# A list scheduler that gives TensorE the units whose inputs have been ready for a while

## The chip, the core and the metric

One Trainium2 chip (trn2), one of its cores, everything in float32. The metric is the device time of one execution in microseconds (us), as the median of several runs. PE is TensorE's matmul side, PEld its weight loads, DVE is VectorE, ACT is ScalarE, POOL is GpSimd, SP is SyncE, which here only issues DMAs.

## What is computed

The input x has 4 x 1024 tokens of 256 channels. It is normalized, and two branches are added to it:

```python
xn = layernorm(x)                                   # (4, 1024, 256), no scale or shift
# branch 1: linear attention with 16 heads of 16, chunks of 128 tokens, and 4 fixed memories
q, k, v = (split(xn @ w.T) for w in (w_q, w_k, w_v)); sq, sk = elu(q) + 1, elu(k) + 1
local  = causal chunked attention: ((sq sk^T * mask) v + sq S) / clip(its row sums), S += sk^T v
coarse = (sq @ sum(memories)) / clip(sq @ sum(norms))
fine   = sum over m of softmax_m(mean over tokens of sq @ norm_m) * (sq @ memory_m) / clip(sq @ norm_m)
p      = sigmoid(w2 @ relu(w1 @ coarse + b1) + b2)  # one number for each token
attn   = (gate * (p * fine + (1 - p) * coarse) + (1 - gate) * local) @ w_o.T
# branch 2: mixture of 8 experts of width 176, the two best of each token, and a shared MLP of width 352
scores = softmax(xn @ gate_weight.T); w = the two largest, divided by their sum
y      = sum over the two of w * (silu(xn @ wg_e.T) * (xn @ wu_e.T)) @ wd_e.T + shared MLP(xn)
out = x + attn + y
```

## The kernel before

**Stages.** The 4096 tokens are 8 blocks of 512 and 32 tiles of 128. First all blocks are normalized, transposed and turned into values and router logits (lines 328 to 416, up to about 54 us). Then the router picks two experts for each token and sorts the token-expert pairs by expert into 71 slot tiles of 128 (`route`, `sort`, lines 419 to 569). The sorted list is inverted with one-hot matmuls: 22 batches, each `invert` (DVE, L581 and L585), `hold` (ACT, L598) and `hold_weights` (POOL, L608), then `add_slots` (PE, tile `found`, L617). The buffers of a batch come from rings of three, so batch k waits for the `add_slots` of batch k-3. After the last batch `inverted` (DVE, L627 to L633) writes the tables `islot` and `wslot`.

**A round of attention,** for token tile n: `scores` (PE, L746, into the tile `quad`), `mask` (4 times DVE, L753), `memory` (PE, L889, into `quad` again), `weigh` (DVE, L899 to L904) and `fine` (2 times DVE, L923), `gate_coarse` (POOL, tile `cg`, L916), `sum_fine` (POOL: three additions, tiles `fm` and `diff`, L936 to L940), `local` (PE, tile `pn`, L772), `local_copy` (ACT, tile `nT`, L784), `back` (PE, tile `pb`, L793 and L799), `weigh_local` (DVE, tile `loc`, L813 to L817), `base` (POOL, `loc`, L827), `update` (PE, L860), `state` (DVE, L872), `add_state` (POOL, L880); then the gate: `turned` (PE, tile `pt2`, L950), `gate_hidden` (PE, tile `ph`, L976), `gate_sum` (DVE, L985 and L987), `gate_out` (ACT, L993 to L996), `blend` (POOL, tile `o`, L1002), and `output` (PE, tile `po`, L1071 and L1075). Beside the rounds run the projections (L649) and the shared MLP (`pg` L1010, `psu` L1030). Once for each of the 4 sequences `batch_weights` makes the softmax over the memories: 4 small matmuls (L695), then a dozen short DVE and ACT operations (L700 to L719); `weigh` reads its result `w5`.

**The expert part,** for slot tile j: `fetch_rows` (POOL, an indirect DMA that gathers 128 rows, tile `xg`, three buffers, L1133), `fetch_weights` (SP, three DMAs, three buffers), `expert_turn` (PE, tile `pte`, L1166), `turn_copy` (ACT, L1173), `expert_hidden` (PE, tile `phe`, L1183), `expert_tanh` (ACT, L1195), `expert_silu` (DVE, L1200 to L1205), `expert_out` (PE, tile `pye`, L1215), `expert_y` (ACT, L1224), `put` (POOL, an indirect DMA that adds 128 rows to `sums` in HBM, L1229).

**The end.** When the last `put` has landed, `residual` and `experts_part` load `sums` (SP). For tiles 0 to 23 `total` (POOL, L1113, 12 of two tiles each) adds them to what `output` left, and `store_two` (SP) stores; for tiles 24 to 31 `output` runs at the very end, with `output_sum` (DVE, L1083) and `store_one` (a DMA that ACT issues, L1117).

**What sets the order.** PE's main work, some 686 units, is first written as a list (`order`): the rounds, with projections, shared MLP and experts mixed in by weight. A unit's place in it is its due time. `plan` (L1357 to L1584) then runs a list scheduler at build time: every function has an engine and an estimated duration (`cost`), a lag until others see its result (`lag`, `landing`), the units that it must wait for (`needs`), and the PSUM banks (a ring of 4) and `wide` tiles (a ring of 3) that it takes. At each step it looks at the first unit of each function, finds for each engine the one with the smallest rank, and calls the one that begins first. The order of those calls is the order of the instructions on every engine, since each engine works its queue in order. A PE unit may not run more than 12 us ahead of the list (`window`). The estimates act on the order alone. The chip keeps its own time, and a unit that is called too early holds up all that is behind it on its engine.

The heart of it before:

```python
ready = max((done[w] for w in waits if w is not None), default=0.0)
begin = max(ready, free[engine])
rank = (begin, due if engine == "PE" else ready)
```

Of the kernel before, what the change touches and what calls it, by code (L numbers as in the profile page):

```python
# [15 lines left out]
NT = 4  # L16
# [6 lines left out]
def linear_attention_moe_kernel(  # L23
# [53 lines left out]
    BPB = S // TB  # L77
# [118 lines left out]
    for e in range(E):  # L196
# [5 lines left out]
        base=0, pattern=[[1, P]], channel_multiplier=-1,  # L202
# [5 lines left out]
        base=0, pattern=[[1, P]], channel_multiplier=-1,  # L208
# [5 lines left out]
        base=0, pattern=[[-HD, HC]], channel_multiplier=1,  # L214
# [3 lines left out]
        base=HD - 1, pattern=[[HD, HC]], channel_multiplier=-1,  # L218
# [14 lines left out]
    spare = count[:, P + 2 * NTT : P + 2 * NTT + 1]  # L233
# [1123 lines left out]
    def plan(order):  # L1357
# [12 lines left out]
            scores: ("PE", 1.10), memory: ("PE", 0.85), local: ("PE", 1.05), back: ("PE", 0.92),  # L1370
            update: ("PE", 0.48), turned: ("PE", 0.45), keys_back: ("PE", 0.45),
            output: ("PE", 2.17), gate_hidden: ("PE", 0.47), project: ("PE", 1.73),
            shared_gate: ("PE", 1.73), shared_up: ("PE", 1.73), batch_weights: ("PE", 3.50),
            expert_turn: ("PE", 0.24), expert_hidden: ("PE", 1.36), expert_out: ("PE", 0.95),
            odd_keys: ("ACT", 0.52), turned_copy: ("ACT", 0.57), keys_copy: ("ACT", 0.62),
            output_copy: ("ACT", 0.40), local_copy: ("ACT", 0.60), gate_out: ("ACT", 0.90),
# [3 lines left out]
            gate_sum: ("DVE", 0.50), blend: ("POOL", 0.78), weigh_local: ("DVE", 1.08),  # L1380
            state: ("DVE", 0.43), projected: ("DVE", 0.74), shared_silu: ("DVE", 0.66),
            shared_hidden: ("DVE", 0.66), expert_silu: ("DVE", 1.00), mean_queries: ("DVE", 1.30),
            gate_coarse: ("POOL", 0.78), sum_fine: ("POOL", 2.80), base: ("POOL", 0.78),
            add_state: ("POOL", 0.80), put: ("POOL", 1.62), fetch_rows: ("POOL", 1.02),
            fetch_weights: ("SP", 0.3), invert: ("DVE", 1.15), hold: ("ACT", 1.00),
            hold_weights: ("POOL", 0.72), add_slots: ("PE", 0.75), inverted: ("DVE", 0.65),
# [11 lines left out]
        def needs(f, n, *more):  # L1398
# [8 lines left out]
                scores: lambda: qs + ks + [(odd_keys, n), (fine, n - 1, NC - 1)],  # L1407
                mask: lambda: [(scores, n), (local, n - 1)],
                memory: lambda: [(mask, n, g) for g in range(NG)],
                weigh: lambda: [(memory, n), (turned, n - 2), (gate_coarse, n - 1)],  # L1410
                gate_coarse: lambda: [(weigh, n), (base, n - 1), (sum_fine, n - 1)],
                fine: lambda: [(weigh, n), (sum_fine, n - 1)],
                sum_fine: lambda: [(fine, n, NC - 1), (gate_coarse, n), (gate_out, n - 2)],
# [66 lines left out]
        rings = {"bank": [None] * 4, "wide": [None] * 3}  # L1480
# [10 lines left out]
        def taken(f, key):  # L1491

            if f is add_slots:
                return ("bank", (inverted, 0)) if key[1] == 0 else None
            if f not in gives_back or f is update and (state, *key[1:]) not in known:
                return None
            ring, last = gives_back[f]
            if f is output and key[1] >= held_from:
                last = output_sum
            return ring, (last, *key[1:])  # L1500

        def longest_free(ring):

            slots = [(-1.0 if u is None else called[u], k)
                     for k, u in enumerate(rings[ring]) if u is None or u in called]
            return min(slots)[1] if slots else None

        queues, due, place, ended = {}, 0.0, 0.0, False
# [29 lines left out]
        known = {op[0] for queue in queues.values() for op in queue}  # L1538
        queues = {f: queue[::-1] for f, queue in queues.items()}
        free = dict.fromkeys(lag, 0.0)  # L1540
        done, called = {}, {}
        window = 12.0
        while any(queues.values()):
            limit = window + min(
                (q[-1][3] for f, q in queues.items() if q and cost[f][0] == "PE"), default=0.0
            )
            best = {}
            for f, queue in queues.items():
                if not queue:
                    continue  # L1550
                key, args, due, place = queue[-1]
                engine = cost[f][0]
                if engine == "PE" and place > limit:
                    continue
                waits = [key for key in needs(*key) if key in known]
                takes = taken(f, key)
                if takes:
                    slot = longest_free(takes[0])
                    if slot is None:
                        continue  # L1560
                    waits += [rings[takes[0]][slot]]
                if any(w is not None and w not in done for w in waits):
                    continue
                ready = max((done[w] for w in waits if w is not None), default=0.0)
                begin = max(ready, free[engine])
                rank = (begin, due if engine == "PE" else ready)
                if engine not in best or rank < best[engine][0]:
                    best[engine] = rank, f
            assert best
            rank, f = min(best.values(), key=lambda b: b[0][0])  # L1570
            begin = rank[0]
            key, args, *_ = queues[f].pop()
            engine, took = cost[f]
            takes = taken(f, key)
            if takes:
                rings[takes[0]][longest_free(takes[0])] = takes[1]
            called[key] = len(called)
            if f is update and (state, *key[1:]) not in known:
                took = 0.0
                done[add_state, *key[1:]] = begin  # L1580
                called[add_state, *key[1:]] = len(called)
            free[engine] = begin + took
            done[key] = begin + took + landing.get(f, lag[engine])
            f(*args)  # L1584


# [98 lines left out]
    for n in range(held_from, NTT):  # L1685
        order += [(1280, output, n, True), (10, store_one, n)]
    planned.append(True)
    plan(order)


# [54 lines left out]
```

## Time and profile before

| | us |
|---|---|
| median of 3 runs (654.38 to 657.39) | 654.52 |
| the profiled execution | 651.07 |
| its span, first to last instruction | 649.4 |
| PE busy | 627.6 (97%) |
| PE weight loads busy | 487.9 (75%) |
| DVE busy | 429.5 (66%) |
| POOL busy | 408.6 (63%) |
| ACT busy | 278.5 (43%) |
| longest groups: L1183 `phe` matmuls / L1215 `pye` / L1071 `po` | 108.0 / 77.9 / 47.0 |
| POOL: scatter L1229 / gather L1133 / first addition of `sum_fine` L936 | 112.6 / 71.4 / 48.2 |

A row of the timeline gives start, duration, engine, line, operation, what is written from what, shapes and a count of merged instructions, and in brackets the idle time before it and what ended it. A float32 matmul stands as two instructions. Ends of matmuls are modelled, so PE shows as busy also where it runs slowly; the distance from the start of one unit to the start of the next is the better measure of what a unit costs.

### The profile page before, as it was taken

The numbers are of one execution on the slowest core, as the hardware profiler recorded it, in microseconds if no ns is written. First come the engines' busy times: TensorE is split into PE (matmuls) and PEld (weight loads), VectorE is DVE, ScalarE is ACT, GpSimd is POOL, SyncE is SP. The second block draws the span as 40 slices with busy tenths as digits, with TensorE's granted clock in tenths as the row PEclk, the third lists the DMA queues.
The fourth block names the chain that finished last, engine by engine and source line by source line (L and its number), as shares of the span: only waits on it lengthen the run. The fifth ranks groups of instructions, "written<-read, shape, count | busy, mean of one in ns | idle before, by whom it ended". The sixth has DMA issues, their size and how long they took to land.

```text
span 649.4 us, 15187 instructions
## 1 busy us (share of the span) xinstructions
PE 627.6 (97%) x5510; PEld 487.9 (75%) x5510; DVE 429.5 (66%) x1205; ACT 278.5 (43%) x676; POOL 408.6 (63%) x456
## 2 busy tenths in 40 slices
PE   4999999989999999999999999999999999999996
PEld 3884467778888877777786777788888886778775
DVE  6837999966665566566656765666655656667751
ACT  3765455444444454334533444333445434344320
POOL 5310055677777876565665665677777498586876
PEclk9999999999999999999999999999999999999999
DMA  9779000156566753443443444346666675564278
GB/s 301 242 238 248 0 1 2 50 168 166 133 152 144 164 129 87 106 107 77 109 118 78 106 107 98 89 106 138 154 151 160 149 161 127 147 164 99 26 225 301
DMA packets 94379, 86.51 MB, mean 133 GB/s; under 512 B 12033, under 2 KB 91905, under 8 KB 94177
## 3 DMA queue, kind: packets, MB, share of 16 engines
q1 hardware_dynamic: 78976, 65.34, 34.5%
q0 software_dynamic: 13632, 18.62, 16.6%
q10 hardware_dynamic: 1696, 1.58, 0.7%
q8 instruction: 44, 0.72, 0.5%
q14 instruction: 31, 0.25, 0.1%
HBM read 67.56 MB, written 23.59 MB: 140 GB/s over the span
## 4 chain that ended last, share of the span: by engine, by line
PE 89%; DVE 6%; ACT 1%; DMA 1%; issue 1%; POOL 0%; DVEq 0%
PE phe L1183 14%; PE pye L1215 11%; PE po L1071 6%; PE psu L1030 6%; PE pg L1010 5%; PE quad L746 5%; PE pn L772 5%; PE pv L407 5%; PE po L1075 4%; PE quad L889 4%; PE pq L649 3%; PE pk L649 3%; PE pte L1166 3%; PE pb L793 2%; PE pb L799 2%; PE found L617 2%
## 5 line engine op out<-in xcount | busy, mean ns | idle before, releaser
L1229 POOL DMA_INDIRECT sums<-y,islot x71 | 112.6, 1585 | 56.5 <-ACT y L1224 16.1
L1183 PEld LDWEIGHTS phe<-turned,wgu 128*128 128x128 f32 (+1 forms) x852 | 102.2, 187 | 14.9 <-issue 12.9
L1183 PE MATMUL phe<-turned,wgu 128*128 128x128 f32 (+1 forms) x852 | 108.0, 276 | 0.0
L1133 POOL DMA_INDIRECT xg<-xns,islot x71 | 71.4, 1006 | 58.0 <-PE pte L1166 43.9
L753 DVE TENSOR_TENSOR sT<-quad,causal 128x512 f32<-128x512 f32 x128 | 79.4, 682 | 21.9 <-PE quad L746 9.5
L1215 PE MATMUL pye<-wdn,hidden 112*128 112x256 f32 (+1 forms) x284 | 77.9, 396 | 0.5
L1200 DVE SCALAR_TENSOR_TENSOR the<-the,phe 128x256 f32<-128x256 f32 x71 | 29.5, 415 | 43.3 <-ACT the L1195 30.0
L1215 PEld LDWEIGHTS pye<-wdn,hidden 112*128 112x128 f32 (+1 forms) x284 | 48.8, 190 | 11.4 <-issue 3.2
L936 POOL TENSOR_TENSOR fm<-fm 128x512 f32<-128x512 f32 x32 | 48.2, 1506 | 4.2 <-DVE fm L923 4.2
L1224 ACT ACTIVATE y<-pye,wslot 128x256 f32<-128x256 f32 x71 | 33.4, 471 | 38.9 <-PE pye L1215 36.2
L1195 ACT ACTIVATE the<-phe 128x256 f32<-128x256 f32 x71 | 27.1, 382 | 51.6 <-PE phe L1183 45.8
L608 POOL TENSOR_TENSOR held<-ones,two 128x213 f32<-128x213 f32 (+1 forms) x22 | 16.3, 748 | 49.5 <-DVE ones L581 49.5
L1071 PE MATMUL po<-wd,h 128*128 128x256 f32 (+1 forms) x192 | 47.0, 380 | 0.0
L1010 PE MATMUL pg<-xnT,wg 128*128 128x512 f32 (+1 forms) x96 | 45.7, 598 | 0.5 <-DVE th L1040 0.5
L1030 PE MATMUL psu<-xnT,wu 128*128 128x512 f32 (+1 forms) x96 | 45.9, 600 | 0.0
L923 DVE TENSOR_TENSOR fm<-quad,rw 128x512 f32<-128x512 f32 x64 | 41.0, 682 | 0.2
L1071 PEld LDWEIGHTS po<-wd,h 128*128 128x128 f32 (+1 forms) x192 | 35.5, 190 | 6.1 <-issue 1.6
L916 POOL TENSOR_TENSOR cg<-coarse,gates 128x256 f32<-128x256 f32 x32 | 30.9, 964 | 13.9 <-DVE coarse L904 11.6
L1173 ACT COPY turned<-pte 128x256 f32<-128x256 f32 x71 | 26.5, 373 | 27.6 <-PE pte L1166 25.6
L1002 POOL TENSOR_TENSOR o<-o,loc 128x256 f32<-128x256 f32 x32 | 29.7, 929 | 7.8 <-ACT o L996 5.8
L772 PE MATMUL pn<-sT,va 128*32 128x128 f32 x1024 | 34.6, 276 | 0.0
L827 POOL TENSOR_TENSOR loc<-loc,cg 128x256 f32<-128x256 f32 x32 | 26.5, 827 | 12.7 <-DVE loc L817 12.0
(200 smaller groups left out, 1329.8 us busy)
## 6 DMA issues: line engine op xcount, KB each, us to landing
wdn<-in_w_down_dram SPq DMA_DIRECT2D x71, 224.0 KB
wgu<-in_w_gate_dram SPq DMA_DIRECT2D x71, 176.0 KB
wgu<-ups SPq DMA_DIRECT2D x71, 176.0 KB
xns<-x SPq DMA_DIRECT2D x8, 512.0 KB
sums<-in_x_dram SPq DMA_DIRECT2D x8, 512.0 KB
x<-in_x_dram SPq DMA_DIRECT2D x7, 512.0 KB
part<-sums SPq DMA_DIRECT2D x12, 256.0 KB
out_dram<-acc SPq DMA_DIRECT2D x12, 256.0 KB
```

Source lines behind the costliest of these rows:

```text
L649: nc.tensor.matmul(pq, w[:, k, c * P : (c + 1) * P], xnT[:, k, :], start=(k == 0), stop=(k == NC - 1),)
L753: nc.vector.tensor_mul(sT, quad[:, g, :].rearrange("p (c t) -> p c t", t=P), causal[:, None, :].to_broadcast([P, NC * 2, P]),)
L772: nc.tensor.matmul(pn[CW * r : CW * (r + 1), q, :], wide[:, i, first : first + CW], st["sT", h // 2][:, c * 2 + h % 2, :], start=True, sto ...
L923: nc.vector.tensor_mul(fm[:, c].rearrange("p g m (r k) -> p g (m r) k", k=HD), quad[:, :, c * KM + KX + KN : (c + 1) * KM].rearrange("p g ...
L936: nc.gpsimd.tensor_add(fm[:, :, 0:2, :], fm[:, :, 0:2, :], fm[:, :, 2:4, :])
L1010: nc.tensor.matmul(pg[:n, :], wg[:, k, f * P : f * P + n], xnT[:, k, :], start=(k == 0), stop=(k == NC - 1),)
L1030: nc.tensor.matmul(pu[:n, :], wu[:, k, f * P : f * P + n], xnT[:, k, :], start=(k == 0), stop=(k == NC - 1),)
L1071: nc.tensor.matmul(po[:, :H], st["h", blk, f][:k, tok], wd[:k, f, :], start=(f == 0), stop=False)
L1133: nc.gpsimd.indirect_dma_start(out=xg, out_offset=None, in_=xns, in_offset=bass.IndirectOffsetOnAxis(ap=islot[:, j : j + 1], axis=0),)
L1183: nc.tensor.matmul(ph[: cols.stop - cols.start, s, :], wgu[:, k].rearrange("p g f -> p (g f)")[:, cols], xgT[:, k, :], start=(k == 0), sto ...
L1215: nc.tensor.matmul(py[:, :H], hT[:n, f, :], wdn[:n, f, :], start=(f == 0), stop=(f == 1))
L1229: nc.gpsimd.indirect_dma_start(out=sums, out_offset=bass.IndirectOffsetOnAxis(ap=islot[:, j : j + 1], axis=0), in_=st.pop(("y", j)), in_of ...
```

## The change

Three things are changed, all in `plan`, so no instruction is added or removed; only their order on the engines moves.

1. Estimates: `batch_weights` counts 0.95 us of PE in place of 3.50, and DVE is held for its result plus 2.2 us, at which time it is done; `weigh` now waits for it. `sum_fine` counts 3.20 us of POOL in place of 2.80.
2. The rank of a PE unit: its begin is taken as no earlier than the time at which its inputs have been ready for a while. "A while" depends on the engine that made the input (`spare`: ACT 0.4, DVE 0.6, POOL 1.5, SP 1.0 us). Among units with the same begin the earlier due one wins, as before.
3. Once a unit is chosen, its begin is worked out anew from its inputs and the ring slot, without the margin.

```diff
-            shared_gate: ("PE", 1.73), shared_up: ("PE", 1.73), batch_weights: ("PE", 3.50),
+            shared_gate: ("PE", 1.73), shared_up: ("PE", 1.73), batch_weights: ("PE", 0.95),
...
-            gate_coarse: ("POOL", 0.78), sum_fine: ("POOL", 2.80), base: ("POOL", 0.78),
+            gate_coarse: ("POOL", 0.78), sum_fine: ("POOL", 3.20), base: ("POOL", 0.78),
...
-                weigh: lambda: [(memory, n), (turned, n - 2), (gate_coarse, n - 1)],
+                weigh: lambda: [
+                    (memory, n), (batch_weights, n // (BPB * NT)), (turned, n - 2), (gate_coarse, n - 1)
+                ],
...
-        done, called = {}, {}
+        done, called, by = {}, {}, {}
+
+        spare = {"PE": 0.0, "ACT": 0.4, "DVE": 0.6, "POOL": 1.5, "SP": 1.0}
...
                 begin = max(ready, free[engine])
-                rank = (begin, due if engine == "PE" else ready)
+                rank = (begin, ready)
+                if engine == "PE":
+                    safe = max((done[w] + by.get(w, 0.0) for w in waits if w), default=0.0)
+                    rank = (max(begin, safe), due)
...
             rank, f = min(best.values(), key=lambda b: b[0][0])
-            begin = rank[0]
...
+            waits = [w for w in needs(*key) if w in known]
             if takes:
-                rings[takes[0]][longest_free(takes[0])] = takes[1]
+                slot = longest_free(takes[0])
+                waits += [rings[takes[0]][slot]]
+                rings[takes[0]][slot] = takes[1]
+            begin = max([free[engine]] + [done[w] for w in waits if w])
...
             done[key] = begin + took + landing.get(f, lag[engine])
+            by[key] = spare[engine]
+            if f is batch_weights:
+                free["DVE"] = max(free["DVE"], done[key]) + 2.2
+                done[key] = free["DVE"]
             f(*args)
```

## The prediction

> **What bounds the kernel now.** I read the busy times first, then PE's own waits, then the timeline where waits lie, and last the end of the run.
>
> ```profile
> PE 627.6 (97%) x5510; PEld 487.9 (75%) x5510; DVE 429.5 (66%) x1205; ACT 278.5 (43%) x676; POOL 408.6 (63%) x456
> ```
>
> PE works 97% of the span, so the sum of its work (the same after the change) sets the time, and an order of units can win only what PE waits. The waits of PE, by the engine that ended them (total, times, longest, in us):
>
> ```profile
> PE pt L385 <- ACT x L367: 8.7, 2, 7.6
> PE pb L793 <- ACT nT L784: 2.4, 2, 1.2
> PE pte L1166 <- DMA xg<-xns,islot: 2.2, 2, 1.4
> PE pte L1166 <- issue: 1.1, 1, 1.1
> ```
>
> The first line is the start, before the planner's part. The rest, with four waits of 0.5 or less, is 7.0 us (2.4 + 2.2 + 1.1 + 1.2): all that this change could take away. The stages, with PE's busy time as the second number:
>
> ```profile
> 80.00:130.00 50.00, 49.37 (x411) 35.32 (x410) 47.41 (x103) 26.03 (x82) 27.05 (x34) 1.00 0.06 17
> 130.00:200.00 70.00, 67.72 (x694) 57.50 (x693) 45.52 (x126) 29.18 (x71) 53.97 (x55) 1.00 0.63 160
> ```
>
> PE's idle time in the second stretch (2.3 us) lies where the experts begin. In the first, DVE (47.41 of 50) is as full as PE: the batches of the inversion. The start of the experts:
>
> ```profile
> 129.05 0.22 DVE L633 COPY wslot<-found 128x71 f32<-128x71 f32 x1
> 129.44 1.23 POOL L1133 DMA_INDIRECT xg<-xns,islot  x1 [2.09 <-DVE wslot L633]
> 131.63 1.08 PE L772 MATMUL pn<-sT,va 128*32 128x128 f32 x32
> 134.16 0.41 PE L1166 MATMUL pte<-ident,xg 128*128 128x128 f32 x2 [1.44 <-DMA xg<-xns,islot]
> 135.79 0.41 PE L1166 MATMUL pte<-ident,xg 128*128 128x128 f32 x2 [0.75 <-DMA xg<-xns,islot]
> ```
>
> The last `add_slots` starts at 127.76, `inverted` ends at 129.27, and POOL, idle for 2.09 us, issues the first gather at once. From that issue to the first `expert_turn` it is 4.72 us. PE has other work until about 132.6 and waits for the rest. And the end:
>
> ```profile
> 627.23 0.29 ACT L993 ACTIVATE prob<-z,b 128x1 f32<-128x1 f32 x1 [2.26 <-DVE ph L987]
> 628.49 0.73 POOL L1002 TENSOR_TENSOR o<-o,loc 128x256 f32<-128x256 f32 x1 [1.74 <-issue]
> 629.18 14.24 POOL L1113 TENSOR_TENSOR acc<-acc,part 128x512 f32<-128x512 f32 x12
> 644.01 0.42 DVE L1083 TENSOR_TENSOR acc<-po,res 128x256 f32<-128x256 f32 x1 [1.74 <-PE po L1075]
> ```
>
> Two chains finish almost together: PE's last `output`, whose sum on DVE begins at 644.01, and POOL's row of 12 `total`, which cannot start before the last `blend` (628.49) and ends at 643.42, with the store of its last two tiles behind it.
>
> **The change, part by part.** I compared the order of instructions that each text builds, engine by engine. 462 of PE's 686 units start after the same amount of PE work as before, and whole stretches of the middle are untouched. The changes lie in the inversion and the start of the experts (75 to 150 us), in ten `scores` and `memory` units moved up by 3 to 7 us (tiles 12, 13, 15, 25, 27 to 29), and in the last rounds.
>
> *The start of the experts.* In the old order po_0 (1.30 + 0.86), memory_2 (0.79), ph_1 (0.39), pn_2 (1.01), pu_2 (0.47) and pb_2 (0.91) follow the last `add_slots`; in the new one they precede it. (These are start-to-start times of the units.) So it starts 5.7 us later, at 133.5. Behind it PE has scores_3 (1.10), the transposition pt2_1 (0.44) and po_1 (2.16), then the first `expert_turn`: 0.24 + 3.70, at 137.4, if nothing is late.
>
> Now the gather. On DVE `inverted` stands behind `weigh_local` of tile 2: pb_2 ends at 133.5, `weigh_local` takes 1.2, `inverted` 0.7, so the table is there by 135.6. On POOL, though, seven operations that used to follow the first four gathers now stand ahead of them: `cg` and `o`, the three of `sum_fine`, `state` and `loc`. memory_2 ends at 130.0; `weigh` (1.73), `gate_sum` (0.6) and `fine` (1.28) bring the tile `fm` at 133.8. Then POOL's queue: `o` until 134.6, `fm` 1.27, `diff` 0.75 and 0.92, `state` 0.76, `loc` 0.86, all durations from the timeline near 118 to 127 us: the gather starts at about 139.3, ten microseconds later than before, while PE's list is only five longer.
>
> How long the gather takes is open from two sides. By the row it is 4.72, but there the weights of three slot tiles landed beside it, and here they will mostly be in. The Trainium skill ("DMA: Bandwidth & Descriptors", section "Anatomy of one DMA — SWDGE (gpsimd) path") fits 2.0 us plus bytes over 436 GB/s; with 128 KB (0.3) and the issue of the usual row (1.0) an estimate of 3.3. By the row PE waits until 144.0, by the page until 142.6. I take 3.7, nearer the page because the contention has gone: 143.0, a wait of 5.6. `expert_hidden` of tile 0 now follows its own `expert_turn` directly; the copy between ends 0.8 to 0.9 after the turn's start (134.61 plus 0.37, from 134.16), against 0.22 of work: 0.7 more. Before, the two waits here were 1.44 and 0.75. Net: 5.6 + 0.7 - 2.2 = +4.1 (page +3.7, row +5.1). Afterwards pte_1 to pte_5 and the first `pye` find their gathers in time, and from there the orders meet again.
>
> A wait this long meets a rule that speaks against the change. The clock:
>
> ```profile
> 10.78 3.73 PE L407 MATMUL pv<-wvg,xnT 128*128 128x264 f32 x8
> 15.69 3.73 PE L407 MATMUL pv<-wvg,xnT 128*128 128x264 f32 x16
> ```
>
> At the start, after 7.6 us of idle, eight matmuls took as long as sixteen a little later: half speed, although the PEclk column shows 1.00. The Trainium skill ("TensorE: Matmul & The Clock Gate", section "HAM oscillation — how this bites in real kernels") warns of any idle gap over about 3.4 us. No gap inside the plan was that long before; by the row of the start the slow stretch lasts some 5 us, a loss of 2.6, by the page's 3.4 us window 1.7, and if the gap doesn't fill such a window, 0. I take +0.5 and keep 0 to 2.6.
>
> *The inversion.* The `add_slots` units come 2 to 6 us later, attention units earlier. DVE builds two of the batches (42, 54) about when PE reaches them, with 2 us for `hold` and `hold_weights` in between: +0.4, from 0 to +1.3. The ring of three does not hold DVE up by my count.
>
> *The middle.* The waits of 1.1 at 342, 1.2 at 533 and 1.1 at 553 us come where PE's own completion signals arrived late, with the same neighbours in both orders; a planner's margin wins little there. PE's work between `local` and `back` grows from 1.43 to 1.72 at the median, which covers the 0.1 to 0.3 by which `nT` was late in some rounds. Units moved up have 3.7 us or more for what must happen before them (four masks take 2.5 plus signals). I take -1.0, from -4.5 (every wait there gone) to +3 (each moved unit half a microsecond late). `batch_weights` moves up by 0.9 us of PE work in two of its four places; its matmuls are 2.1 us in all on PE and stay, DVE's dozen operations run as before: within this. The new estimate of `sum_fine` costs nothing by itself: the chip's three additions stay 3.0 (1.51 + 0.73 + 0.74).
>
> *The end.* ph_31 goes behind po_24: 2.2 us of PE work later. Ahead of its `gate_out` ACT now also has the store of tile 24, which waits for that `output_sum`; cheap, some 0.4. So the last `blend` comes at 630.7, the twelve `total` end at 645.7, and their last store, 3.6 us behind before (643.4 to 647.0 in the DMA records), lands at 649.3; the last store of the other chain landed at 647.7. So +1.5, from 0 (if the store is quicker) to +2.3. The last `put` comes earlier by some 5 us, which only gives the loads more room.
>
> **Sum**, against the profiled execution: 651.07 + 4.1 + 0.5 + 0.4 - 1.0 + 1.5 = 656.6. The median of the runs was 3.45 above the profiled execution, so 660.0. My count at the start takes every POOL operation one after another and at its worst place; I shade it by 0.7: **659.3**.
>
> **Rivals.** About 0.5%, 3.3 us, is what a measurement of this kernel tells from no change.
>
> *The start costs half* (within 0.5%). The gather is issued at 137.5, because POOL is ahead of my count, and takes 3.3: PE waits until 140.8 or 3.4, no loss of clock, and the end costs 0.5. Then 3.4 + 0.7 - 2.2 + 0.5 - 1.0 = +1.4, 655.9. For it: POOL works only 27.05 of 50 us before 130. Against: its operations there hang one on another.
>
> *The margins pay* (not slower). One mechanism: PE no longer stands behind a unit that is just too early, so the waits after 140 us, 4.8 in all with those under 0.5, go. Price -4.8, less what the start costs. It decides if the first gather is issued within 7 us of the last `add_slots` starting there, or 1.7 later than PE's list can cover; then -4.8 + 1.7 = -3.1, 651.4. Against it: those places stand in the same order.
>
> *Attention waits for DVE.* If moved-up `scores` and `memory` are each 0.5 late (ten of them) and DVE falls behind in the inversion by 1.3 where I count 0.4, it is +6 on top: 665.
>
> **Chances.** Forecast 0.57 (656.5 to 662.5), half the start 0.25, margins pay 0.10, DVE 0.08. Slower by over 0.5%: most of the first (0.51), 0.02 of the second, all of the last, 0.61. Within: 0.06 + 0.23 + 0.04 = 0.33. Faster by over 0.5%: 0.06. The range leaves out most of the third and the tail of the last: 654.0 to 663.0.
>
> **What would show it.** Right: PE's wait for the first `xg` grows to 4 to 6.5 us near 138 to 143; the first gather stands behind `loc` on POOL and starts near 139; `total` starts near 631 to 632 plus the shift of all; PE's other waits stay near 4 to 5 us. Wrong: a first gather issued within 4 us of the last `add_slots`; new waits of PE for DVE at moved `scores` or `memory`; or an end that follows PE's last matmul as closely as before (5.4 us from 643.97 to the end of the span). A halved spacing of matmuls behind the gap would decide the clock.

## The result, and the profile after

The changed kernel takes 656.45 us (median of 20 runs, 655.25 to 657.88), the kernel before 654.45 on the same chip (20 runs, 651.82 to 658.38). The ratio is 1.0029 (95%: 1.0015 to 1.0043), so +1.9 us (1.0 to 2.8). The forecast was 659.3, +4.8: the direction holds, the size does not.

| us | before | after |
|---|---|---|
| median | 654.45 | 656.45 |
| profiled execution / its span | 651.07 / 649.4 | 657.71 / 656.0 |
| profiled execution less median | -3.4 | +1.3 |
| mean granted clock of PE (share of full speed), profiled | 0.998 | 0.994 |

The two profiles alone differ by 6.6 us, more than the forecast; the medians by 2.0. The third row is what the account below turns on. The mean clock in the last one also counts a stretch at half clock behind PE's last matmul, which costs PE nothing: of the clock withheld, it is 1.3 us before (all there is) and 2.5 of 4.2 after.

The longest waits of PE after, but for the start of the run (the columns are total, times, longest, in us):

```profile
PE pte L1166 <- DMA xg<-xns,islot: 3.7, 1, 3.7
PE po L1071 <- DVE hidden L1205: 1.3, 1, 1.3
PE phe L1183 <- PE pte L1166: 0.9, 1, 0.9
PE pt L950 <- POOL o L1002: 0.8, 2, 0.5
```

The two waits of `back` for `nT` (2.4) and the 1.1 of `expert_turn` are gone. In their place stand one wait of 3.7 for the first gather and a handful of small ones, 1.3 for `hidden` (at 513 us) the largest. The start of the experts, from the timeline of the changed kernel (POOL and PE):

```profile
138.35 0.73 POOL L827 TENSOR_TENSOR loc<-loc,cg 128x256 f32<-128x256 f32 x1
139.26 1.22 POOL L1133 DMA_INDIRECT xg<-xns,islot  x1 [0.17 <-issue]
...
142.36 0.54 PE L1166 MATMUL pte<-ident,xg 128*128 128x128 f32 x2 [3.70 <-DMA xg<-xns,islot]
143.36 2.81 PE L1183 MATMUL phe<-turned,wgu 128*128 128x128 f32 x12 [0.46 <-ACT turned L1173]
...
147.78 1.55 PE L1183 MATMUL phe<-turned,wgu 128*128 128x128 f32 x12
```

The gather is issued at 139.26 behind `loc`, as forecast (139.3), and PE waits for it until 142.36. The same twelve `phe` matmuls then take 2.81 us the first time and 1.55 the second. The windows of the changed kernel (behind the window's width stands PE's busy time; the number ahead of the last two is the granted clock) say why:

```profile
138.00:142.40 4.40, 0.70 (x5) 0.30 (x4) 0.89 (x2) 0.37 (x1) 3.62 (x5) 1.00 0.45 139
142.40:146.00 3.60, 3.14 (x14) 2.77 (x15) 0.00 (x0) 0.37 (x1) 1.56 (x2) 0.53 0.37 109
146.00:150.00 4.00, 4.00 (x43) 3.59 (x42) 3.16 (x12) 1.66 (x6) 2.31 (x3) 1.00 0.47 131
```

After the gap the clock is 0.53 for 3.6 us, then full again. And the end, from the timeline of the changed kernel:

```profile
635.92 0.72 POOL L1002 TENSOR_TENSOR o<-o,loc 128x256 f32<-128x256 f32 x1 [3.32 <-issue]
636.61 14.22 POOL L1113 TENSOR_TENSOR acc<-acc,part 128x512 f32<-128x512 f32 x12
...
648.80 0.42 DVE L1083 TENSOR_TENSOR acc<-po,res 128x256 f32<-128x256 f32 x1 [1.74 <-PE po L1075]
```

PE's last sum is 4.8 later than before (644.01), the twelve `total` start 7.4 later (629.18): POOL's chain is now the last.

To divide the 6.6 us between the profiles, set the starts of PE's units against the PE work that lies before each, and read how far the changed kernel is behind at equal work: +0.6 at 126 us (the first loads), +5.5 at 170, +4.8 at 630, and the spans end 6.6 apart. So the start of the experts cost 4.9, the middle gave 0.7, the end cost 1.8.

### The profile page after: what moved, and what is told of

Same layout as the page of the kernel before. It is cut to its first block, busy times and chain, and to the rows that moved or that the text cites. A ratio compares the mean times of both kernels' runs of the same rounds, so it can differ in the third digit from the quotient of the medians.

```text
span 656.0 us, 15193 instructions
## 1 busy us (share of the span) xinstructions
PE 629.8 (96%) x5510; PEld 488.8 (75%) x5510; DVE 429.9 (66%) x1205; ACT 279.8 (43%) x676; POOL 408.6 (62%) x456
## 5 line engine op out<-in xcount | busy, mean ns | idle before, releaser
L1183 PE MATMUL phe<-turned,wgu 128*128 128x128 f32 (+1 forms) x852 | 109.6, 279 | 1.3 <-PE pte L1166 0.9
L936 POOL TENSOR_TENSOR fm<-fm 128x512 f32<-128x512 f32 x32 | 45.6, 1426 | 3.5 <-DVE fm L923 3.5
L916 POOL TENSOR_TENSOR cg<-coarse,gates 128x256 f32<-128x256 f32 x32 | 29.5, 923 | 19.6 <-DVE coarse L904 16.9
```

The lines of the kernel that those rows point to most:

```text
L936: nc.gpsimd.tensor_add(fm[:, :, 0:2, :], fm[:, :, 0:2, :], fm[:, :, 2:4, :])
L1183: nc.tensor.matmul(ph[: cols.stop - cols.start, s, :], wgu[:, k].rearrange("p g f -> p (g f)")[:, cols], xgT[:, k, :], start=(k == 0), sto ...
```

## The experiments

The runs came on five chips, A to E, and the kernel before was run on each of them too; differences are against that median, as ratio times median, with the 95% interval. "Clock" is the median over the timed runs of the mean granted clock of each.

| chip | kernel | median | before | difference | clock |
|---|---|---|---|---|---|
| A | before again | 655.12 | 654.96 | -0.1 (-1.2 to 1.0) | 0.994 |
| A | start only | 657.91 | 654.96 | +3.8 (2.2 to 5.4) | 0.993 |
| A | middle only | 648.46 | 654.96 | -6.7 (-7.9 to -5.5) | 1.000 |
| A | end only | 657.16 | 654.96 | +2.3 (1.6 to 3.0) | 0.993 |
| B | before, filled | 649.97 | 651.65 | -1.7 (-2.5 to -0.8) | 0.998 |
| B | after, filled | 654.07 | 651.65 | +2.2 (1.3 to 3.1) | 0.998 |
| B | middle, later | 647.43 | 651.65 | -3.9 (-5.5 to -2.4) | 0.996 |
| B | start and middle | 653.23 | 651.65 | +2.2 (1.2 to 3.3) | 0.993 |
| C | after again | 655.36 | 651.50 | +3.8 (2.3 to 5.2) | 0.992 |
| C | after without its end | 653.54 | 651.50 | +1.9 (0.9 to 2.9) | 0.993 |
| C | rank alone | 653.28 | 651.50 | +1.7 (0.7 to 2.7) | 0.995 |
| C | middle and landing | 645.12 | 651.50 | -6.8 (-9.2 to -4.5) | 0.998 |
| D | start only, 2nd | 654.04 | 651.51 | +2.6 (1.7 to 3.5) | 0.993 |
| D | without the start | 644.44 | 651.51 | -7.5 (-9.3 to -5.7) | 1.000 |
| D | gather first | 653.42 | 651.51 | +1.6 (0.5 to 2.6) | 0.994 |
| D | after, 3rd | 654.81 | 651.51 | +3.2 (2.1 to 4.2) | 0.992 |
| E | late margin, landing | 647.05 | 655.47 | -7.5 (-9.2 to -5.8) | 1.000 |

**Chip A: the three places one by one.** The theory "ordinary waits" said that the profiled execution of before was a lucky one, with some 3 us of waits fewer than the ordinary, and that the margins take those away; two rivals put the 3 us at the start of the experts or outside the plan. The kernel before was run again unchanged, and the new rank was let act in one place at a time, with the old estimates:

```diff
# start only
+                    if (inverted, 0) not in done:
+                        begin = max(begin, safe)
# middle only
+                    if (inverted, 0) in done and (expert_turn, NST - 1) not in done:
+                        begin = max(begin, safe)
# end only
+                    if (expert_turn, NST - 1) in done:
+                        begin = max(begin, safe)
                     rank = (begin, due)
```

> The kernel before, unchanged, for a second profile. The profiled execution that the forecast started from took 651.07 us, below the lowest of the 20 timed runs (651.82 to 658.38, median 654.45). Theory 'ordinary waits' (the ordinary execution has some 3 us of waits inside the plan that the first profile did not have, and the margins take them away): a profile near 654.5 has PE waits behind the start of the experts that add up to 8 or more in place of 4.8, the start of the experts and the end as in the first. Rival 'ordinary start' (the ordinary execution loses its 3 us at the start of the experts, by a later gather or a halved clock, and the new order loses them too, so it only looks dearer against the first profile): PE's wait for the first two xg is 4 to 6 us, or the granted clock is near 0.994, and the middle has 4.8 as before. Rival 'elsewhere' (loads at the very start or the DMAs at the very end): neither; the first matmul or the tail behind the last matmul is 3 us later.

> The margin acts only until the inversion is done, and the estimates are as before: the start of the experts stands as in the changed kernel (last add_slots 5.7 us of PE work later), the middle and the end as before. Against the median before: 'ordinary waits' +4.0 to +4.8 us (4.4 by the difference of the two profiles), a PE wait of 3.5 to 4 for the first xg and a first expert_hidden at half speed (2.6 in place of 1.3). 'Ordinary start' +0.5 to +1.5. 'Elsewhere' +4.4 as well.

> The margin acts only from the end of the inversion to the last expert_turn, with the estimates as before: the ten moved scores and memory units and their neighbours, start and end as before. Against the median before: 'ordinary waits' -3.5 to -4.5 us (what is missing between 4.4 + 1.8 and the measured 1.9). 'Ordinary start' and 'elsewhere' -1.0 to +0.5.

> The margin acts only after the last expert_turn, with the estimates as before: ph_31 stands behind po_24, and memory_29, scores_30 and memory_30 come 3 to 5 us earlier. All theories but one: +1.5 to +2.0 us (1.8 by the two profiles), with the row of twelve total starting 2 to 3 us later. 'Elsewhere', if the ordinary execution ends late anyway because of the DMAs: 0 to +0.5.

The second profile of before was again below its median (652.81 against 655.12), at a clock of 0.999, and PE's waits behind the start of the experts were only 0.9 us more than in the first, not the 3 or more that "ordinary waits" asked for: that theory lost its footing. But the timed runs told something that the page could not: their clock has a median of 0.994, from 0.991 to 0.999, and in the 35 runs of before on this chip those up to 0.9925 have a median of 655.6 and those above 0.9965 of 653.8. An ordinary execution of before already loses clock, it seems. Start (+3.8; +4.0 to +4.8 by "ordinary waits") and end (+2.3; +1.5 to +2.0) came near what was expected; the middle gave -6.7, more than the -3.5 to -4.5 expected and more than all the waits behind the start of the experts (4.0 in the first profile), and its five timed runs after the profiled one had a clock of 1.000. Its PE waits, where before had 2.2, 2.4 and 1.1:

```profile
PE pte L1166 <- DMA xg<-xns,islot: 1.0, 1, 1.0
PE pte L1166 <- ACT prob L994: 0.9, 1, 0.9
...
PE pb L793 <- ACT nT L784: 0.3, 1, 0.3
```

In this kernel `update` of tile 2 (0.47 us) goes ahead of the first `expert_turn`, so a part of the gain may be the clock at the start and not the middle.

**Chip B: the clock.** Two kernels give PE work while it waits (transpositions that are written over at once; the changed kernel has `{0: 34}` in place of `{0: 14, 1: 8}`), and one keeps the start of the experts exactly as before:

```diff
         xg = st.pop(("xg", j))
+        for _ in range({0: 14, 1: 8}.get(j, 0)):
+            nc.tensor.transpose(pt[:, 0, :], ident, ident)
# middle, later
+                    if (expert_turn, 8) in done and (expert_turn, NST - 1) not in done:
# start and middle
+                    if (expert_turn, NST - 1) not in done:
+                        begin = max(begin, safe)
```

> The kernel before, with 14 extra 128x128 transpositions of the identity ahead of those of the first expert_turn and 8 ahead of those of the second (about 1.5 and 0.9 us at 0.11 each), which are written over at once: PE works on while it waits for the first two gathers. Theory 'clock' (in an ordinary execution of the kernel before, PE's clock is halved for some microseconds at the start of the experts: the timed runs have a mean granted clock of 0.994 at the median, the two profiled ones 0.998 and 0.999; so the 3.45 us between profile and median, which the forecast added as a constant, is in good part a loss that the changed kernel pays only once): the clock of the timed runs rises to 0.998 or more and the time falls by 1.5 to 2.6 us, to 652.4 to 653.5. Rival 'waits' (the difference is late signals all over the plan, the clock only goes with them): clock 0.994 to 0.998, time within 0.7 us of before.

> The changed kernel, with 34 extra transpositions of the identity (3.7 us) ahead of those of the first expert_turn. 'Clock': the first expert_hidden takes 1.33 us in place of 2.65, the clock rises from 0.991 to 0.998 or more and the time falls from 656.45 by 1.3 to 2.6 us; against the kernel before -0.6 to +0.6. 'Waits': the time stays at +1.5 to +2.3.

> As the kernel with the margin in the middle alone (which gave -6.5), but from the ninth expert_turn on: the start of the experts is now exactly that of before, where the other had update of tile 2 ahead of the first expert_turn and pb_2 ahead of the second. 'Clock': the gain falls to what the waits at 342, 533 and 553 us are worth, -3.2 to -4.0, and the clock of the timed runs is near 0.994, not 1.000. 'Waits': -6 to -7, since all of it is in the middle.

> The margin acts until the last expert_turn, with the estimates as before: start and middle as in the changed kernel, the end as before. 'Clock': with the late start the clock loss is there whatever the middle does, so +3.0 (start alone) and -3.4 (middle without the clock) give -0.4, from -1.2 to +0.5, at a clock near 0.993. 'Waits' (the parts add): +3.0 - 6.5 = -3.5.

Filling the kernel before raised its clock from 0.994 to 0.998 and took 1.7 us off, though the gathers landed no sooner (5.2 us from issue to the first `expert_turn`): "clock" holds there. "Middle, later" fell to -3.9, as "clock" said: about 2.8 of the -6.7 sat at the start, as far as two chips can be compared. "After, filled" had its clock back (0.998), and its first `expert_hidden` was at full speed, but at +2.2 it missed the -0.6 to +0.6 of "clock" and fell where "waits" had it. Both took the +1.9 of the result's chip as their mark; against the changed kernel on chips C and D, where before has nearly the same median as here, it is 0.7 to 1.3 lower. That is a comparison across chips, so for the changed kernel the price of the clock is not shown in time. "Start and middle" gave +2.2 where "clock" said -0.4 and "waits" -3.5: both missed. With the late start the middle gains little.

**Chip C: does the end, or do the estimates, make up the rest?**

```diff
# after without its end
+                    if (expert_turn, NST - 1) not in done:
+                        begin = max(begin, safe)
# rank alone: the changed kernel less its estimates
-            shared_gate: ("PE", 1.73), shared_up: ("PE", 1.73), batch_weights: ("PE", 0.95),
+            shared_gate: ("PE", 1.73), shared_up: ("PE", 1.73), batch_weights: ("PE", 3.50),
-            gate_coarse: ("POOL", 0.78), sum_fine: ("POOL", 3.20), base: ("POOL", 0.78),
+            gate_coarse: ("POOL", 0.78), sum_fine: ("POOL", 2.80), base: ("POOL", 0.78),
# middle and landing: middle only, and
-        landing = {fetch_rows: 2.0, put: 2.9, residual: 2.5, experts_part: 2.5}
+        landing = {fetch_rows: 3.7, put: 2.9, residual: 2.5, experts_part: 2.5}
```

(In "rank alone" `weigh` does not wait for `batch_weights` and DVE is not held either.)

> The changed kernel again, as the mark for the next two on one chip, and for a second profile. Theory 'interplay' (start +3.8, middle -6.7 and end +2.3 taken alone don't add to the measured 1.9: with the late start the middle gains only 2 to 4 of its 6.7, because the part of it that is the clock at the start can't be had) and its rival 'estimates' (the new estimates of batch_weights and sum_fine make up what is missing) both expect +1.0 to +2.8 against the kernel before, at a clock near 0.991.

> The changed kernel with the margin off once the last expert_turn is planned: ph_31 and the last rounds stand as before, estimates as changed. If the end costs here what it costs alone (+2.3), the time is 2.3 below the changed kernel: -1.3 to +0.5 against before. 'Estimates' expects this too. If the end is hidden in the changed kernel, +1.9. 'Interplay' has the kernel with start and middle and the old estimates (+2.2 measured) as its mark: +1.2 to +3.3 here too.

> The new rank with its margins, and the estimates as before (batch_weights 3.50, sum_fine 2.80, no hold of DVE, weigh does not wait for batch_weights). 'Estimates': start and middle with the old estimates measured +2.2, the end alone +2.3, so +3.5 to +5.5 here, and the new estimates take 2.6 of it away. 'Interplay': within 0.8 us of the changed kernel, +1.1 to +2.7.

> The margin in the middle alone (-6.7 by its ratio), and the planner is told that a gather takes 3.7 us until it has landed in place of 2.0: the first expert_turn comes 1.4 us of PE work later and the second 3.3, behind back of tile 2 and scores of tile 3. If PE's waits for the first two gathers (1.0 and 0.9 in the profile of the middle alone) and the clock are all that is left there, the clock stays at 1.000 and the time falls by another 1 to 2 us, -7.7 to -8.7 against before. If something else holds PE there (the copies or the DVE steps of the first expert tiles), it stays at -6 to -7.

The same changed kernel is +3.8 here. Without its end it is 1.9 better, so the end costs within the whole about what it costs alone. The new estimates do not help, against both theories: without them it is 2.1 better (the +1.7 lies in the range that "interplay" gave, but not within 0.8 of the changed kernel). "Middle and landing" had no clear gain over the middle alone (-6.8; -7.7 to -8.7 expected).

**Chip D: the parts on one chip.**

```diff
# without the start: rank alone, and
+                    if (inverted, 0) in done:
+                        begin = max(begin, safe)
# gather first: the changed kernel, and
-                sum_fine: lambda: [(fine, n, NC - 1), (gate_coarse, n), (gate_out, n - 2)],
+                sum_fine: lambda: [(fine, n, NC - 1), (gate_coarse, n), (gate_out, n - 2)]
+                + [(fetch_rows, 0) for _ in range(1) if n == 2],
```

> The start alone once more (margin only until the inversion is done), now on one chip with the whole change and with the change less its start. On the first chip it was +3.8 (2.2 to 5.4). If parts add on one chip: whole change less 'without start', to within 1.5 us. 'Clock charged twice' (the forecast took 5.0 for the start against a profile without clock loss, and an ordinary execution of before has 1.7 of that loss already): +2.8 to +3.8. Rival 'start costs what was forecast': +5.0, with the median of the profile pair at 4.4.

> The new rank only from the end of the inversion on, estimates as before: middle and end as changed, the start of the experts as before but for update of tile 2 ahead of the first expert_turn. Middle alone measured -6.7 and -3.9 (with the start exactly as before), the end +2.3: if they add, -4.4, at least -1.6, at a clock of 0.998 or more. If the margins in the middle only pay while the end stays as before, 0.

> The changed kernel with sum_fine of tile 2 made to wait in the plan for the first gather: on POOL the gather is then ahead of fm and the two diff, which the forecast named as what puts it off (issued at 139.26 in the profile, 2.8 after its table is written). Forecast's step right: the gather is issued near 136.8, PE's wait for xg falls from 3.7 to 1.0 to 1.5, the clock rises to 0.995 or more, and the time falls by 2.5 to 3.5 against the changed kernel. If the late add_slots and not POOL's queue is what counts, it falls by less than 1.

> The changed kernel once more, as the mark for the three others on this chip: it measured +1.9 (1.0 to 2.8) on one chip and +3.8 (2.4 to 5.2) on another. Between +1.5 and +4 here, clock 0.991 to 0.993, PE's wait for the first xg 3.6 to 3.9 in the profile.

The parts do not add: the whole less "without the start" is 10.7, the start alone 2.6. The profiles say where 8.1 us of span between the two come from: -1.0 before the plan (the first loads), 4.8 at the start of the experts (+5.3 against +0.5 on the first profile of before), 0.7 in the middle, 3.6 at the end. The end was not the same in both. In "without the start", with the old estimates:

```profile
623.79 4.59 POOL L1113 TENSOR_TENSOR acc<-acc,part 128x512 f32<-128x512 f32 x4
628.35 0.72 POOL L1002 TENSOR_TENSOR o<-o,loc 128x256 f32<-128x256 f32 x1
629.03 9.68 POOL L1113 TENSOR_TENSOR acc<-acc,part 128x512 f32<-128x512 f32 x8
```

Four `total` run while POOL waits for the last `blend`; in the changed kernel all twelve stand behind it (POOL idle for 3.32). From the start of PE's last sum to the end of the span it is 3.5 us here (640.49 to 644.0), 7.2 in the changed kernel (648.80), 5.4 before (644.01). These two differ in the start as well; chip C has the pair that differs in the estimates alone. There "rank alone" has the four `total` ahead and 3.5 us behind the start of PE's last sum, the changed kernel 7.1; since its last sum starts 1.5 later, 2.0 remain, the 2.1 of the medians. So the new estimates have a price, and it lies in the order of POOL at the end. The old ones don't prevent it by themselves: in "end only" all twelve stand behind the last `blend` too (POOL idle for 4.15).

"Gather first" did what it should on POOL, and missed in time:

```profile
136.70 1.22 POOL L1133 DMA_INDIRECT xg<-xns,islot  x1 [0.18 <-issue]
...
140.47 1.27 POOL L936 TENSOR_TENSOR fm<-fm 128x512 f32<-128x512 f32 x1
...
141.33 0.41 PE L1166 MATMUL pte<-ident,xg 128*128 128x128 f32 x2 [2.86 <-DMA xg<-xns,islot]
```

Issued 2.6 us sooner than in the first profile after, the gather needs 4.63 us from issue to `expert_turn` in place of 3.10: the slot weights now move beside it (265 GB/s from 138 to 140; in the changed kernel on this chip it is 87, and the gather takes 3.21). PE's wait falls by 1.0, the time by 1.6 against the changed kernel on this chip, not by 2.5 to 3.5.

**Chip E: the best version, and a third profile of before** (the margin from the end of the inversion on, old estimates, `fetch_rows` landing 3.7).

> What the runs point to as the best: the margin from the end of the inversion on, estimates as before (that gave -7.5), and a gather counted with 3.7 us in place of 2.0 (which took away PE's waits for the first two gathers beside the margin in the middle). If PE's waits there (1.5 and 1.0 in the profile of the first of the two) are what is left, another -1 to -2: -8.5 to -9.5 against before, clock 1.000.

> A third profile of the kernel before. On the two chips where its median is 654.5 to 655 its profiles have two PE waits of back for nT near 533 and 553 us, 2.4 together; on the chips where its median is 651.5, the kernels with the same middle (before filled, and the second run of the start alone) have none. Theory 'chips': on a chip with a median near 651.5 the profile has none of these waits (up to 0.4), on one near 654.5 it has 2.4. Rival: the waits stand in it whatever the median.

The combined kernel gives -7.5, no more than without the landing: PE's waits for the gathers are gone, but 2.4 us of waits of `back` (for `nT`, and 1.0 for nothing that the profile names) came elsewhere. It and "without the start" are the best of the study, 1.1% below the kernel before. The third profile of before fell on a chip with a median of 655.47 and has the waits for `nT` (2.7); whether a chip with 651.5 lacks them was not seen. This profile, though, caught what the timed runs had only hinted at. Windows of this execution of before:

```profile
134.00:136.00 2.00, 1.06 (x10) 0.89 (x9) 0.44 (x1) 1.28 (x4) 1.50 (x2) 1.00 0.24 63
136.00:138.00 2.00, 2.00 (x12) 2.00 (x11) 0.00 (x0) 0.37 (x1) 1.82 (x3) 0.51 0.22 66
138.00:140.00 2.00, 2.00 (x14) 2.00 (x14) 0.00 (x0) 0.05 (x1) 1.92 (x3) 0.64 0.21 66
```

and the same stretch in the profile that the forecast was made from:

```profile
136.00:138.00 2.00, 2.00 (x20) 2.00 (x19) 0.00 (x0) 0.37 (x1) 1.81 (x3) 1.00 0.23 66
138.00:140.00 2.00, 2.00 (x20) 1.95 (x19) 1.04 (x4) 0.65 (x2) 1.92 (x3) 1.00 0.42 99
```

26 instructions in place of 40 in four microseconds, in the old order, after gaps of 2.02 and 0.94 where the first profile had 1.44 and 0.75. Busy stays 2.00 in both, so only the clock and the counts show it.

## Why the prediction missed

*The step that failed: "The median of the runs was 3.45 above the profiled execution, so 660.0."* The terms ahead of it add up to 5.5, and between the two profiles the change did cost 6.6. What failed is the step from the profile to the median: the 3.45 was taken for a constant that the changed kernel would have too, and its profile lies above its median, so the medians are only 2.0 apart. Its profiled executions lie +1.3, +0.1 and -1.0 from their medians; those of before -3.4, -2.3 and -2.4. (That the sum without the 3.45, 656.6, comes so close to the median of 656.45 is in part luck: the profile that it forecast took 657.71.) One part of the 3.45 is shown, the halved clock at the start of the experts, which the first profile of before did not have: filling that gap gave 1.7 (0.8 to 2.5) and moved the clock from 0.994 to 0.998. The forecast charged the changed order with a long gap and its clock, on top of a constant that held the clock loss of the old order: twice the same thing. What the other half of the 3.45 is stays open; the timed runs leave no trace. The clock is not all of it: the third profile of before has the halved stretch and is still 2.4 below its median. Nor is one profiled execution more than one draw: those of the other kernels here lie from 2.7 below to 2.7 above their medians.

*The start,* forecast +5.0 with the inversion and the clock: 4.9 between the profiles, so right against the profile. Within it the gather's issue was right to 0.1; the wait was 3.7 and not 5.6, since PE's list ended 1.2 us later than counted (138.66; 0.6 of it the first loads) and the gather took 3.10, the Trainium skill's side ("DMA: Bandwidth & Descriptors", "Anatomy of one DMA — SWDGE (gpsimd) path": an estimate of 3.3 with the issue) and not the row's 4.72. "Gather first" fits traffic as the reason: 4.63 with weights beside it, 3.21 without on the same chip. The clock was +1.3 in the first `expert_hidden` alone (2.65 from start to start against 1.33), not +0.5. Against the ordinary execution of before the start costs +3.8 and +2.6: there the old order pays clock as well. Near the start of the experts the clock withheld is 0, 0, 1.7, 1.7 and 3.4 us in the five profiles that have the old order there (three of before, "end only", "middle, later"), and 1.7 (twice) or 3.4 (six times) in the eight that have the whole late start.

*The middle,* forecast -1.0: 0.7 gained between the profiles. But the reason was wrong. "The waits of 1.1 at 342, 1.2 at 533 and 1.1 at 553 us come where PE's own completion signals arrived late, with the same neighbours in both orders": they did go (3.5 us), and new small ones took most of it back. Nor were the neighbours the same: near 533 us the new order puts an `expert_out` (1.03) between `local` and `back`. At 342 and 553 the unit just ahead is the old one; what made the signals late there was not found. With the old start and the margin in the middle the gain is 3.9.

*The end,* forecast +1.5: +1.8 between the profiles, +2.3 alone; `total` starts 2.6 later than PE's shift explains, forecast 2.2. The last `put` did not come some 5 us earlier but 2.8 later (620.58 against 617.81). That the new estimates, with the margin on everywhere, decide whether four `total` fit in ahead of the last `blend` was not seen: "the new estimate of `sum_fine` costs nothing by itself" was wrong in its effect on the order.

*The rivals.* "The start costs half" has the number (655.9), not the mechanism: its gather at 137.5 and wait without clock loss did not happen. "The margins pay" was judged at 0.10 because the neighbours stay the same; alone, in the middle, it took off 6.7 with the clock at the start and 3.9 without. "Attention waits for DVE" didn't happen: the new waits for `sT` are 0.4.

*What stays open.* On chips D and C, where before has 651.5, the change costs 3.2 and 3.8, on the result's chip, with 654.45, 1.9. The two waits for `nT`, 2.4 us, which the margin removes (0.3 left in "middle only"), are in the profiles of the slower chips and in no kernel with the old middle that was profiled on the faster ones ("before, filled", "start only, 2nd"); that would be the difference, but the kernel before itself was not profiled there. Nor is it explained why the middle gains so little beside the late start in timed runs (+2.2 with it, +2.6 and +3.8 without), when in the profile of that kernel it gained 2.0 (+5.7 at 170 us, +3.7 at 630).

## What to carry to other kernels

The distance between a profiled execution and the median is not a constant to be added: find what the profile lacks (the mean clock of the timed runs shows part of it here) before charging the same thing to the change. A margin that is meant for the long middle of a plan should be kept out of its seams, where one stage waits for the last unit of another: the same rule gave -3.9 in the middle and +2.6 to +3.8 at the start. And an estimate in a planner that costs nothing in time can still move what stands ahead of what at the end.

## What the hardware showed unexpectedly

The halved clock comes in portions of a fixed length. In all twenty profiles the trace's clock rows change only at whole multiples of 3.413 us from the first row, which lies 13 to 16 us into the run: after 35 to 37 of them near the start of the experts, after 184 to 187 at the end. Between 130 and 150 us the clock withheld is 0, 1.71 or 3.41 us, that is none, one or two such windows at half speed.

What brings it on is PE's idle time within one window of this grid, not the length of a gap. Two neighbouring windows of before, and two of "middle only", cut at the grid:

```profile
131.40:134.81 3.41, 1.97 (x41) 1.66 (x40) 3.16 (x10) 0.79 (x2) 1.47 (x2) 1.00 0.87 242
134.81:138.22 3.41, 2.66 (x24) 2.49 (x24) 0.48 (x2) 1.45 (x5) 3.18 (x4) 1.00 0.29 90
...
133.92:137.34 3.42, 1.53 (x13) 1.38 (x13) 1.73 (x7) 1.61 (x5) 1.71 (x2) 1.00 0.47 117
137.34:140.75 3.41, 3.41 (x18) 3.41 (x17) 0.45 (x2) 0.82 (x3) 2.78 (x3) 0.50 0.21 64
```

In before the waits of 1.44 and 0.75 us fall into two windows, and the clock stays. In "middle only" two waits of 0.86 and 1.04 fall into one, 1.89 idle, and the next window is halved. Counted so over the twenty profiles, from the first clock row to PE's last matmul, thirteen windows at full clock had 1.55 to 3.41 us of idle time and a halved one behind them; no other window at full clock had more than 1.56, and none of those was followed by a halved one. So in this kernel the edge lies near 1.55 of 3.41 us, as exactly as modelled ends of matmuls allow ("end only" with 1.55 fell on one side, the second profile of before with 1.56 on the other). A halved window with 0.76 us or more of idle time was followed by a second (seven times), one with 0.46 or less was not (thirteen times). This also says why the new order pays in each of its profiles and the old one in some: a gap of 3.7 us leaves at least half of itself, 1.85, in one window wherever the grid falls, while the waits of the old order, 1.6 to 3.1 us in all and mostly in two pieces, can stay under the edge.

The length and the fixed grid agree with the Trainium skill ("TensorE: Matmul & The Clock Gate", "What's actually happening"), which has a free-running window of 3413 ns. Its rule of thumb ("HAM oscillation — how this bites in real kernels"), no idle gaps over about 3.4 us, was not enough here. And the PEclk of 1.00 beside the slow matmuls at the very start of the run is no reading of full speed: the trace has no clock row there (the first of before begins at 15.35 us), and the page shows what has no row as 1.00.
